# A convolution with spectral products and a recurrent layer: the start's loads and stores on two queues, and other buffers for the next image's statistics

## The chip, the cores and the metric

The kernel runs on one core of a Trainium2 chip. The metric is device time in microseconds (us) of one execution; lower is better. The engines are TensorE (PE in the profile, its weight loads PEld), VectorE (DVE), ScalarE (ACT), GpSimd (POOL) and SyncE (SP). SP, ACT and POOL issue DMAs; each has a queue of its own.

## The reference, cut to what matters

x is 4 images x 64 channels x 256 x 256, float32. Two layers with residuals follow one another, each after a group norm `_gn` over pairs of channels of one image:

```python
x = x + _L0_conv_ref(_gn(x), w1, w_dw, w_out, ln_w, ln_b)
x = x + _L1_conv_ref(_gn(x), w_ih, w_hh, b_ih, b_hh)
```

The first layer is a 1x1 convolution to 384 channels, a depthwise 3x3 convolution, a split into q, k and v of 128 channels, the circular convolution of q and k in patches of 8 x 8 (by FFTs), a layer norm over the channels, a product with v, and a 1x1 convolution back to 64 channels. The second is a GRU that runs along the image's columns.

What matters here is that `_gn` needs mean and variance of a whole image before its first value can be normalized.

## The kernel before, in words

**The program's order.** Every instruction is kept in program order on its engine (`InOrder`; all of them therefore carry line L157 in the profile, and rows are told apart by their tiles). Semaphores and the places of tiles come from the tile framework. A pool with `bufs=n` lends n buffers for a tag; a new tile waits until a buffer is free. A pool that is closed gives its memory to what is allocated later, which then waits for the last readers of the old tiles.

**The start (lines 214 to 257).** `bt` holds the taps as matrices, `wd` the depthwise weights; PE makes of them the matrices `ts` (100 partitions x 384 x 64), ACT copies them out of PSUM, and three DMAs on POOL's queue store them to `t_all` in HBM (3200 KB each). Meanwhile SP loads image 0 in eight pieces `xc` of 128 partitions x 4096 (three buffers), two DMAs a piece: `piece` yields partitions 0 to 63 (channels of the image's upper half), then 64 to 127. VectorE takes BATCH_NORM_STATS2 of each piece's eight stretches into `bn0` and aggregates into `st0`. `norm_of_pieces` makes scale and shift `sc0` of it. Then ACT issues the GRU's weight loads (`wi`, `wh`, `bias_sb`).

**The blocks (lines 273 to 693).** 32 blocks (n) of 32 columns, eight an image. Each holds its input in four tiles `xq` (loaded on POOL's queue, normalized by ACT or VectorE). In the loop over n:
- `pointwise(n, 0, unit)`, 16 units: matmuls into the ring of PSUM banks `psring`, copied to `h` by ACT or VectorE.
- `finish(n - 1)`: the block before is completed in four steps u: `residual` loads x into a work tile `xr` (SP), `gate` transposes and multiplies (work tiles `y`), `project` multiplies by w_out, adds to `xr`, takes its statistics and stores it to x1 (`store`, SP). The last project waits in `pending`, its store in `later`.
- `circular(n, 0, beside)`: four steps sp. Each transforms q and k (`transform`, with matrices `t` that SP streams back from `t_all`, four buffers), copies q to a work tile on ACT and forms two work tiles `pr` of products on VectorE; then it calls `beside(sp)`. `flush()` runs what is pending: after step 0 the last project of block n - 1, after step 2 the `inverse` of the first two steps (matmuls of `pr` by `g_sb`, copied to `z`).
- `pointwise(n, 1, unit)`, `circular(n, 1, beside)` with the first statistics of `layer_norm(n)`, `pointwise(n, 2, unit)` with the loads of the next `xq`, and `values` with the rest of the layer norm and the next `normalize`.

**Work tiles.** `work` lends from one pool of seven buffers (tag `wk`, 128 x 1024 float32). `q`, `k`, `pr`, `xr`, `y`, `lnm` and the next image's `seen` all come from it. The layer norm's own statistics `lnst` (128 x 768) are in the pool `big`, one buffer.

**The next image's statistics.** In the 24 blocks n < 24, `look(n, k, t)` loads a quarter (four columns of each half) of the matching piece of the next image on POOL's queue, in two DMAs, and `count(n, k, t)` takes two BATCH_NORM_STATS2 of it. `seen0` is looked at before `circular(n, 0)` and counted in its step 1; `seen1` is looked at before `pointwise(n, 1)`, counted and looked at anew at units 8 and 14, and counted for the last time in `circular(n, 1)`.

**The second layer (from line 700)** follows with pools of its own.

Of the kernel before, what the change touches and what calls it, by code (L numbers as in the profile page):

```python
# [19 lines left out]
P = 128  # L20
# [63 lines left out]
def norm_of_pieces(nc, st, t, psum, eps, sc):  # L84

    m_all, d, total, mean = t[:, 128:136], t[:, 136:144], t[:, 144:145], t[:, 145:146]
    nc.vector.tensor_copy(m_all, st[:, :, 0])
    nc.vector.tensor_reduce(total, m_all, mybir.AxisListType.X, ALU.add)  # L90
    yield
    pm = psum()
    nc.tensor.matmul(pm, lhsT=t[:, 0:P], rhs=total, start=True, stop=True)
    nc.vector.tensor_copy(mean, pm)
    nc.vector.tensor_tensor(d, m_all, mean.to_broadcast([P, 8]), ALU.subtract)
    nc.vector.tensor_tensor(d, d, d, ALU.mult)
    nc.vector.tensor_tensor(d, d, st[:, :, 1], ALU.add)
    nc.vector.tensor_reduce(total, d, mybir.AxisListType.X, ALU.add)
    yield
    pv = psum()  # L100
    nc.tensor.matmul(pv, lhsT=t[:, 0:P], rhs=total, start=True, stop=True)
    nc.scalar.activation(sc[:, 1:2], pv, AF.Sqrt, bias=eps, scale=1.0)
    nc.vector.reciprocal(sc[:, 1:2], sc[:, 1:2])
    nc.vector.scalar_tensor_tensor(sc[:, 0:1], mean, -1.0, sc[:, 1:2], ALU.mult, ALU.mult)
    yield
# [57 lines left out]
def tile_conv_then_gru(  # L163
# [42 lines left out]
    def piece(of, b, i, w, n):  # L206

        for half in range(2):
            w0 = half * (W // 2) + i * (W // 16) + w
            yield slice(half * C, (half + 1) * C), of[b, :, w0 : w0 + n, :].rearrange("c w h -> c (w h)")  # L210
# [6 lines left out]
    with tc.tile_pool(name="xa", bufs=3) as xa, tc.tile_pool(name="sta", bufs=1) as sta, tc.tile_pool(  # L217
        name="bps", bufs=1, space=PSUM
    ) as bps:
        bt = sta.tile([P, 32, HALO], F32, tag="bt", name="bt")  # L220
        wd = sta.tile([P, HID], F32, tag="wd", name="wd")
        for i in range(4):
            nc.scalar.dma_start(bt[32 * i : 32 * i + 9], taps[i])
            nc.sync.dma_start(wd[32 * i : 32 * i + 9], w_dw)
        avg4 = sta.tile([P, 1024], F32, tag="avg4", name="avg4_0")
        nc.sync.dma_start(avg4[:, 0:P], avg2)
        ts = sta.tile([HALO, 3 * P, NS], F32, tag="ts", name="ts")
        banks = bps.tile([P, 8, 512], F32, tag="b", name="psb")
        for i in range(32):
            kind, s = i // 16, i % 16  # L230
            c0, num = 2 * P * kind, 2 * P - P * kind
            ps = banks[0:HALO, 4 * (i % 2) : 4 * (i % 2) + 4, 0:num]
            for k in range(4):
                at = slice(32 * k, 32 * k + 9)
                nc.tensor.matmul(
                    ps[:, k],
                    lhsT=bt[at, i, :],
                    rhs=wd[at, c0 : c0 + num],
                    start=True,
                    stop=True,  # L240
                    tile_position=(32 * k, 0),
                )
            nc.scalar.copy(ts[:, c0 : c0 + num, 4 * s : 4 * s + 4], ps.rearrange("p s c -> p c s"))
        for i in range(3):
            nc.gpsimd.dma_start(
                t_all[i].rearrange("n p k -> p n k"),
                ts[:, i * P : (i + 1) * P].rearrange("p (n c) k -> p n (c k)", n=8),
            )
        for i in range(8):
            xc = xa.tile([P, 4096], F32, tag="xc", name=f"xc_{i}")  # L250
            for at, of in piece(x, 0, i, 0, 16):
                nc.sync.dma_start(xc[at], of)
            for k in range(8):
                nc.vector.bn_stats(bn0[:, k, :], xc[:, 512 * k : 512 * k + 512])
            nc.vector.bn_aggr(st0[:, i, :], bn0)
        for _ in norm_of_pieces(nc, st0, avg4, lambda: banks[:, 0, 0:1], eps, sc0[:, 0]):
            pass
    wi = const.tile([P, 9, C], F32, tag="wi", name="wi")
# [14 lines left out]
    with ExitStack() as s:  # L273
# [14 lines left out]
        def work(name, shape=(P, 1024)):  # L288
            return wk.tile(list(shape), F32, tag="wk", name=name)

        h = big.tile([HALO, P, NP], F32, tag="h", name="h")
        z = big.tile([P, NP, NS], F32, tag="z", name="z")
        v = big.tile([P, NP, NS], F32, tag="v", name="v")
        xq = {}

        def load(n, jq):
# [159 lines left out]

        def layer_norm(n):

            st = big.tile([P, 2, NP // 2, 6], F32, tag="lnst", name=f"lnst_{n}")

            def statistics(a, p0, p1):

                for p in range(p0, p1):
                    nc.vector.bn_stats(
                        st[:, a, p, :],
                        z[:, 2 * p : 2 * p + 2, 32 * a : 32 * a + 32].rearrange("p n f -> p f n"),
                    )

            for i in range(4):
                statistics(0, 16 * i, 16 * i + 16)  # L470
                yield
            statistics(1, 0, 8)
            yield
            statistics(1, 8, 50)
            yield
            statistics(1, 50, NP // 2)
            m = work(f"lnm_{n}", (P, 8, NP))
            total, mean, d, var, rstd = m[:, 0], m[:, 1], m[:, 2:4], m[:, 4], m[:, 5]
            by = st.rearrange("p a i (e k) -> p a (i e) k", e=2)
            nc.vector.tensor_tensor(total, by[:, 0, :, 1], by[:, 1, :, 1], ALU.add)  # L480
            yield
            pm = psum()
            nc.tensor.matmul(pm[:, 0, 0:NP], lhsT=hh_sb, rhs=total, start=True, stop=True)
            nc.vector.tensor_copy(mean, pm[:, 0, 0:NP])
            nc.vector.tensor_tensor(
                d,
                by[:, :, :, 1],
                mean.rearrange("p (x n) -> p x n", x=1).to_broadcast([P, 2, NP]),
                ALU.subtract,
            )  # L490
            nc.vector.tensor_tensor(d, d, d, ALU.mult)
            nc.vector.scalar_tensor_tensor(d, by[:, :, :, 2], 1.0 / 32, d, ALU.mult, ALU.add)
            nc.vector.tensor_tensor(var, d[:, 0], d[:, 1], ALU.add)
            yield
            pv = psum()
            nc.tensor.matmul(pv[:, 0, 0:NP], lhsT=hh_sb, rhs=var, start=True, stop=True)
            nc.scalar.activation(rstd, pv[:, 0, 0:NP], AF.Sqrt, bias=eps, scale=1.0)
            nc.vector.reciprocal(rstd, rstd)
            yield
            for u in range(4):  # L500
                for g in range(2):
                    at = slice(g * NJ + 16 * u, g * NJ + 16 * u + 16)
                    for part, what in ((mean, ALU.subtract), (rstd, ALU.mult)):
                        nc.vector.tensor_tensor(
                            z[:, at, :],
                            z[:, at, :],
                            part[:, at].rearrange("p (n x) -> p n x", x=1).to_broadcast([P, 16, NS]),
                            what,
                        )
                    yield  # L510
# [82 lines left out]
                    xr[g * C : (g + 1) * C],  # L593
                )

        def look(n, k, t):

            for at, of in piece(x, n // 8 + 1, n % 8, 4 * k, 4):
                nc.gpsimd.dma_start(t[at], of)

        def count(n, k, t):
            for i in range(2):
                nc.vector.bn_stats(bn0[:, 2 * k + i, :], t[:, 512 * i : 512 * i + 512])
            if k == 3:
                nc.vector.bn_aggr(st0[:, n % 8, :], bn0)

        def finish(n):

# [14 lines left out]
        for n in range(NBLK + 1):  # L623
# [4 lines left out]
            if n == NBLK:  # L628
                for _ in norm:
                    pass  # L630
            if n:
                finish(n - 1)
            if n == NBLK:
                flush()
                later.pop()()
                break
            more = n // 8 + 1 < B
            if more:
                seen = work(f"seen0_{n}")
                look(n, 0, seen)  # L640
            circular(n, 0, lambda sp: count(n, 0, seen) if more and sp == 1 else None)
            if more:
                seen = work(f"seen1_{n}")
                look(n, 1, seen)
            for unit in range(16):
                pointwise(n, 1, unit, unit in (5, 8, 11, 14))
                if more and unit in (8, 14):
                    count(n, unit // 7, seen)
                    look(n, unit // 7 + 1, seen)
            flush()  # L650
            norm = layer_norm(n)

            def beside(sp):
                next(norm)
                if more and sp == 1:
                    count(n, 3, seen)

            circular(n, 1, beside)
            image = None
# [264 lines left out]
```

## Time and profile before

| what | value |
|---|---|
| runs of the kernel before | 5904.98, 5915.67, 5931.4 us |
| median | 5915.67 us |
| the profiled execution: own time | 5924.77 us |
| the profiled execution: span from first to last instruction | 5923.0 us |
| granted TensorE clock | 0.992 |
| data moved by DMA | 818.09 MB, mean 138 GB/s |
| DMA packets' time on SP's queue (q1), share of 16 engines | 39.9% |
| DMA packets' time on POOL's queue (q0), share of 16 engines | 9.5% |

The profiled execution took 1.8 us more than its span. In the order of time the start lasts to about 140 us, the blocks to about 4330 us, the second layer to the end. A row of the profile reads: start, duration, engine, line, operation, tile written <- tiles read, shape, count, and in brackets how long the engine had stood idle and what ended that. An engine's name with a q is its sequencer, which issues DMAs. A busy share is an average over stages with different limits.

### The profile page before, as it was taken

Reading aid. Unit: us, or ns where it says so; the run is one execution under the profiler, and the core shown is the slowest. Engines: PE = TensorE matmul, PEld = TensorE weight load, DVE = VectorE, ACT = ScalarE, POOL = GpSimd, SP = SyncE. Lnnn points to the kernel's source line nnn. Section 1 sums busy time; section 2 is a strip of 40 time slices with the busy share of each in tenths; the row PEclk is TensorE's granted clock in tenths of the full one; section 3 lists DMA queues with packets and bytes.
Section 4 is the critical chain, followed back from the end, with each engine's and each line's share of the span. In section 5 each row is a group of like instructions: output and inputs, shape, how many; then the busy total and the mean of one; then the engine's idle time right before and its main releaser. Section 6 shows DMA issues by size and latency. Waiting matters only on the chain. (4 is left out here: it accounts for less than half of the span.)

```text
span 5923.0 us, 279366 instructions
## 1 busy us (share of the span) xinstructions
PE 5513.2 (93%) x127196; PEld 4736.6 (80%) x127196; DVE 4090.4 (69%) x9592; ACT 3466.3 (59%) x4604; POOL 499.7 (8%) x797
## 2 busy tenths in 40 slices
PE   2999999999999999999999999999979999999998
PEld 1888887888887888778878887887868888888887
DVE  2676776777667777776767776666766666676666
ACT  2556565665655666556566665656645555555555
POOL 0000000000000000000000000000001211121211
PEclk9999999999999999999999999999989999999999
DMA  8455555555555555555555545444454444444442
GB/s 223 132 160 142 154 151 155 152 141 160 151 147 149 157 155 141 147 162 146 153 146 154 145 127 142 133 131 136 123 119 112 113 112 110 113 114 113 111 113 78
DMA packets 561921, 818.09 MB, mean 138 GB/s; under 512 B 41352, under 2 KB 435372, under 8 KB 559676
## 3 DMA queue, kind: packets, MB, share of 16 engines
q1 hardware_dynamic: 520152, 633.59, 39.9%
q0 software_dynamic: 37776, 165.24, 9.5%
q8 instruction: 996, 16.32, 1.2%
q10 hardware_dynamic: 2808, 1.38, 0.1%
q14 instruction: 189, 1.55, 0.1%
HBM read 622.46 MB, written 144.05 MB: 129 GB/s over the span
## 5 line engine op out<-in xcount | busy, mean ns | idle before, releaser
L157 PEld LDWEIGHTS psring<-h,t 100*32 100x32 f32 x40960 | 1334.8, 115 | 300.4 <-issue 176.2
L157 PE MATMUL psring<-h,t 100*32 100x128 f32 x40960 | 1445.7, 274 | 113.0 <-issue 39.4
L157 PE MATMUL psring<-w_sb,xq 64*100 64x128 f32 x24576 | 1396.9, 271 | 58.1 <-POOL xq L157 44.1
L157 PEld LDWEIGHTS psring<-w_sb,xq 64*100 64x100 f32 x24576 | 1352.7, 163 | 117.9 <-issue 48.1
L157 ACT COPY h<-psring 100x1024 f32<-100x1024 f32 x1274 | 1204.0, 1026 | 156.8 <-PE psring L157 150.4
L157 DVE TENSOR_TENSOR pr<-psring,q 128x512 f32<-128x512 f32 (+1 forms) x576 | 463.0, 856 | 299.1 <-PE psring L157 230.8
L157 DVE BATCH_NORM_STATS2 lnst<-z 128x6 f32<-128x64 f32 x4096 | 544.8, 212 | 117.6 <-ACT z L157 117.6
L157 DVE TENSOR_TENSOR z<-z,lnm 128x1024 f32<-128x1024 f32 x512 | 612.6, 1217 | 8.7
L157 ACT COPY q<-psring 128x1024 f32<-128x1024 f32 x256 | 259.2, 1013 | 586.5 <-PE psring L157 351.2
L157 ACT ACTIVATE n<-n,bias_sb 128x288 f32<-128x288 f32 (+7 forms) x510 | 259.8, 509 | 572.7 <-DVE n L157 572.7
L157 ACT COPY z<-psring 128x2048 f32<-128x2048 f32 x128 | 238.9, 1866 | 463.3 <-PE psring L157 458.3
L157 PE MATMUL psring<-pr,g_sb 32*64 32x512 f32 x8192 | 497.5, 602 | 5.9 <-issue 5.7
L157 ACT ACTIVATE y<-psring,ln_sb 128x512 f32<-128x512 f32 x512 | 371.9, 780 | 199.7 <-PE psring L157 196.0
L157 DVE COPY h<-psring 100x1024 f32<-100x1024 f32 x262 | 320.3, 1223 | 193.5 <-PE psring L157 189.4
L157 PE MATMUL psni<-st,wi 64*64 64x144 f32 (+7 forms) x12240 | 440.9, 270 | 7.4 <-issue 6.7
L157 PE MATMUL pshr<-st,wi 64*64 64x144 f32 (+7 forms) x12240 | 434.0, 270 | 13.4 <-DVE st L157 12.9
L157 PE MATMUL pshz<-st,wi 64*64 64x144 f32 (+7 forms) x12240 | 439.4, 270 | 3.9 <-issue 3.5
L157 DVE TENSOR_TENSOR g<-xn,n 128x288 f32<-128x288 f32 (+7 forms) x510 | 217.4, 426 | 325.5 <-ACT n L157 325.5
L157 POOL TENSOR_TENSOR raw<-raw,st 128x512 f32<-128x512 f32 x256 | 303.4, 1185 | 1212.0 <-DVE st L157 522.0
L157 DVE TENSOR_TENSOR y<-psring,y 128x1024 f32<-128x1024 f32 x256 | 312.2, 1220 | 122.1 <-ACT y L157 118.8
L157 PEld LDWEIGHTS pshr<-st,wi 64*64 64x64 f32 x12240 | 362.1, 133 | 16.5 <-issue 16.0
L157 PEld LDWEIGHTS psni<-st,wi 64*64 64x64 f32 x12240 | 363.1, 133 | 14.3 <-issue 11.4
(97 smaller groups left out, 6984.0 us busy)
## 6 DMA issues: line engine op xcount, KB each, us to landing
t<-t_all SPq DMA_DIRECT2D x768, 400.0 KB
xq<-in_xh POOLq DMA_DIRECT2D x128, 800.0 KB, 4.6
xr<-in_x SPq DMA_DIRECT2D x256, 256.0 KB
x<-xr SPq DMA_DIRECT2D x256, 256.0 KB
seen<-in_x POOLq DMA_DIRECT2D x192, 256.0 KB, 4.1
raw<-x SPq DMA_DIRECT2D x128, 256.0 KB
raw<-x SPq DMA_DIRECT2D x256, 128.0 KB
xt<-xn SPq DMA_DIRECT2D x256, 128.0 KB
```

Source lines behind the costliest of these rows:

```text
L157: return self.tc.keep_in_program_order(got(*args, **kwargs))
```

## The change

Three parts. First, `bt` is loaded on SP's queue, behind `wd`, where it was on ACT's. Second, the two halves of each `xc` piece go out on SP's and POOL's queue, and the stores of `ts` come after them in the program, each cut into two halves of four matrices, one for each queue. Third, the next image's statistics: `lnst` is one tile for all blocks, and its first 512 values a partition serve as `seen`, two columns at a time, for the first half of a piece; the second half goes through one work tile `four`, four columns at a time. There are six looks a block (12 DMAs) instead of four (8 DMAs), and still eight BATCH_NORM_STATS2. The first look stands before `finish(n - 1)`; counts are at steps 0 and 3 of `circular(n, 0)`, at unit 8 and after unit 15 of `pointwise(n, 1)`, and in step 1 of `circular(n, 1)`.

```diff
         for i in range(4):
-            nc.scalar.dma_start(bt[32 * i : 32 * i + 9], taps[i])
             nc.sync.dma_start(wd[32 * i : 32 * i + 9], w_dw)
+            nc.sync.dma_start(bt[32 * i : 32 * i + 9], taps[i])
...
-        for i in range(3):
-            nc.gpsimd.dma_start(
-                t_all[i].rearrange("n p k -> p n k"),
-                ts[:, i * P : (i + 1) * P].rearrange("p (n c) k -> p n (c k)", n=8),
-            )
         for i in range(8):
             xc = xa.tile([P, 4096], F32, tag="xc", name=f"xc_{i}")
-            for at, of in piece(x, 0, i, 0, 16):
-                nc.sync.dma_start(xc[at], of)
+            for queue, (at, of) in zip((nc.sync, nc.gpsimd), piece(x, 0, i, 0, 16)):
+                queue.dma_start(xc[at], of)
...
+        for i in range(3):
+            for k, queue in enumerate((nc.sync, nc.gpsimd)):
+                queue.dma_start(
+                    t_all[i, 4 * k : 4 * k + 4].rearrange("n p k -> p n k"),
+                    ts[:, i * P + 64 * k : i * P + 64 * k + 64].rearrange("p (n c) k -> p n (c k)", n=4),
+                )
...
+        lnst = big.tile([P, 2, NP // 2, 6], F32, tag="lnst", name="lnst")
...
-            st = big.tile([P, 2, NP // 2, 6], F32, tag="lnst", name=f"lnst_{n}")
+            st = lnst
...
-        def look(n, k, t):
-
-            for at, of in piece(x, n // 8 + 1, n % 8, 4 * k, 4):
+        seen = lnst.rearrange("p a i k -> p (a i k)")[:, 0:512]
+
+        def look(n, w, t):
+
+            for at, of in piece(x, n // 8 + 1, n % 8, w, t.shape[1] // H):
                 nc.gpsimd.dma_start(t[at], of)
-        def count(n, k, t):
-            for i in range(2):
-                nc.vector.bn_stats(bn0[:, 2 * k + i, :], t[:, 512 * i : 512 * i + 512])
-            if k == 3:
-                nc.vector.bn_aggr(st0[:, n % 8, :], bn0)
+        def count(n, w, t):
+            for i in range(t.shape[1] // 512):
+                nc.vector.bn_stats(bn0[:, w // 2 + i, :], t[:, 512 * i : 512 * i + 512])
...
+            if n < NBLK and n // 8 + 1 < B:
+                look(n, 0, seen)
             if n:
                 finish(n - 1)
...
+            def beside_first(sp):
+                if more and sp in (0, 3):
+                    count(n, 2 * (sp // 3), seen)
+                    look(n, 2 * (sp // 3) + 2, seen)
+
+            circular(n, 0, beside_first)
             if more:
-                seen = work(f"seen0_{n}")
-                look(n, 0, seen)
-            circular(n, 0, lambda sp: count(n, 0, seen) if more and sp == 1 else None)
-            if more:
-                seen = work(f"seen1_{n}")
-                look(n, 1, seen)
+                four = work(f"seen_{n}")
+                look(n, 8, four)
             for unit in range(16):
                 pointwise(n, 1, unit, unit in (5, 8, 11, 14))
-                if more and unit in (8, 14):
-                    count(n, unit // 7, seen)
-                    look(n, unit // 7 + 1, seen)
+                if more and unit == 8:
+                    count(n, 4, seen)
+                    look(n, 6, seen)
+                    count(n, 8, four)
+                    look(n, 12, four)
+            if more:
+                count(n, 6, seen)
...
                 if more and sp == 1:
-                    count(n, 3, seen)
+                    count(n, 12, four)
+                    nc.vector.bn_aggr(st0[:, n % 8, :], bn0)
```

## The prediction

> **What bounds the kernel now.** I read the profile from the whole to the part: busy shares first, then the start in stretches and in order of time, then the 32 blocks, then one block with the next image's statistics beside one without.
>
> The page's first line gives the engines' busy time and share of the span.
>
> ```profile
> PE 5513.2 (93%) x127196; PEld 4736.6 (80%) x127196; DVE 4090.4 (69%) x9592; ACT 3466.3 (59%) x4604; POOL 499.7 (8%) x797
> ```
>
> TensorE (PE) is the bound almost everywhere. A change that leaves PE's work alone gains only where PE stands still: before its first block, and in gaps inside the blocks. Next, the start in stretches (columns: length; busy time of PE, PEld, DVE, ACT and POOL with instruction counts; clock, DMA share, GB/s):
>
> ```profile
> 25.00:45.00 20.00, 17.91 (x148) 7.61 (x146) 11.18 (x20) 16.84 (x19) 1.77 (x2) 1.00 1.03 216
> 55.00:80.00 25.00, 0.00 (x0) 0.00 (x0) 12.55 (x22) 0.00 (x0) 0.94 (x1) 1.00 1.01 250
> 90.00:97.00 7.00, 0.00 (x0) 0.00 (x0) 4.40 (x8) 0.00 (x0) 0.00 (x0) 1.00 1.00 330
> 136.00:142.00 6.00, 1.63 (x16) 1.63 (x18) 0.00 (x0) 1.72 (x1) 0.34 (x2) 1.00 1.03 326
> ```
>
> The DMA engines are full in all four, yet move different amounts. The x loads alone (SP, half the partitions at a time) get 216 GB/s; with the matrices' stores beside them on POOL's queue, 250; the stores nearly alone, 330; the xq loads (128 partitions, POOL) beside t loads (SP), 326. What follows the loads, in order of time:
>
> ```profile
> 92.60 4.84 DVE L157 BATCH_NORM_STATS2 bn<-xc 128x6 f32<-128x512 f32 x8 [4.40 <-DMA xc<-in_x]
> ...
> 128.52 7.54 SPq L157 DMA_DIRECT2D t<-t_all  x4
> 129.31 2.16 POOL L157 DMA_DIRECT2D xq<-in_xh  x4 [73.37 <-DMA wi<-in_w_ih]
> 138.14 1.72 ACT L157 ACTIVATE xq<-xq,sc 128x1600 f32<-128x1600 f32 x1 [35.95 <-DMA wi<-in_w_ih]
> 140.37 0.96 PE L157 MATMUL psring<-w_sb,xq 64*100 64x128 f32 x6 [39.83 <-POOL xq L157]
> ```
>
> The last x piece lands at 92.60. The last store is issued at 54.94 and takes 73.5 us, so it lands at 128.4; only then do SP and POOL go on, because the tiles that they load lie where ts lay. (The wi load that is named ends in the same stretch; SP's t load does not need it.) PE's first block follows 12 us after the last store. So the start is set by two bodies of DMA: 16.8 MB of x, then the rest of 9.8 MB of stores.
>
> Now the blocks: blocks 8 to 22 (with the next image's statistics) and 24 to 30 (without), each counted from its first copy out of psring into h.
>
> ```profile
> 1174.40:3136.80 1962.40, 1898.63 (x37506) 1600.00 (x37504) 1409.30 (x3280) 1186.70 (x1188) 102.64 (x247) 0.99 0.55 151
> 3269.70:4173.00 903.30, 876.73 (x17502) 739.35 (x17500) 620.71 (x1464) 553.65 (x555) 18.51 (x58) 1.00 0.49 137
> ```
>
> That is 1962.40 / 15 = 130.83 us a block against 903.30 / 7 = 129.04. DVE has 5.3 us more work a block with the statistics (93.95 against 88.67) but idles over 36 us in either; 1.79 us reach the end. Where, VectorE shows in order of time in circular(n, 0) of block 16 and of block 29:
>
> ```profile
> 2255.89 1.23 DVE L157 TENSOR_TENSOR pr<-psring,q 128x1024 f32<-128x1024 f32 x1 [1.12 <-PE psring L157]
> 2260.45 1.29 DVE L157 TENSOR_TENSOR pr<-psring,q 128x512 f32<-128x512 f32 x2 [3.33 <-DMA x<-xr]
> 2261.65 1.28 DVE L157 TENSOR_TENSOR xr<-psring,xr 128x512 f32<-128x512 f32 x2
> ...
> 2268.31 2.42 DVE L157 TENSOR_TENSOR pr<-psring,q 128x1024 f32<-128x1024 f32 x3 [0.19 <-issue]
> ```
>
> ```profile
> 3951.97 2.42 DVE L157 TENSOR_TENSOR pr<-psring,q 128x1024 f32<-128x1024 f32 x3 [1.12 <-PE psring L157]
> ...
> 3957.46 2.42 DVE L157 TENSOR_TENSOR pr<-psring,q 128x1024 f32<-128x1024 f32 x3 [0.15 <-PE psring L157]
> 3961.10 2.42 DVE L157 TENSOR_TENSOR pr<-psring,q 128x1024 f32<-128x1024 f32 x3 [1.22 <-PE psring L157]
> ```
>
> In block 16 the second product of step sp = 0 waits 3.33 us until the store of an earlier xr lands: seen0 has shifted the seven work buffers by one, so that product gets xr's buffer. From first to third group it takes 12.42 us against 9.13. Block 16 lasts 128.5 us, block 29 126.7.
>
> **The start, step by step.** *x loads.* Each piece's halves go out on SP and POOL together. SP begins x behind the wd, bt and avg loads, at about 6 us (bt's four are 0.46 MB); POOL at 1.5, with 1.0 MB by then at 216. Left: 16.8 + 0.5 - 1.0 = 16.2 MB. The rate of two queues of loads that fill 128 partitions lies between 250 (the second queue a side stream) and 326 (xq beside t); I take 310, nearer to the row of loads. 16.2 / 0.310 = 52 us: x ends at 58, not 92.6. VectorE keeps up: 8 x (4.84 + 0.37) = 42 us.
>
> The trace thus says that a second queue adds to 216 GB/s. The Trainium skill says otherwise ("DMA: Bandwidth & Descriptors", Rules for kernel authors): it advises against splitting a transfer into two for disjoint partition halves, since both run on the same 16 engines. By that rule x would still end at 92.6 and the start would be slower by 13. The same skill ("SBUF — State Buffer", the DMA port swizzle) lets 64 partitions reach half of the ports, 8 x 27.2 = 218 GB/s, which 216 agrees with; it adds that two transfers can't be fused, which 250 and 326 speak against.
>
> *Stores.* They are now queued behind x on both queues, in halves of 1200 packets of 4 KB. SP's t loads, of the same shape, run ten packets at a time in the trace (from 129.5 to 133.5 us), POOL's stores some 15. So the busiest DMA engines get 1200 / 10 + 7 x 12 = 204 packets, where all on POOL gave 7 x 24 = 168: the split balances worse. A packet took 0.193 us (88 to 95 us) to 0.253 (120 to 129); at 0.225 that is 46 us, and the last store lands at 58 + 46 = 104 instead of 128.4: **-24 us**. Ends: 326 and 0.193 give 55 + 39 = 94 (-34); 250 and 0.253 give 71 + 52 = 123 (-5).
>
> Behind them all stays as it is: xq, normalize, PE 12 us later. ACT's 13 weight loads, issued from 100.69 to 130.65 now, come before the first normalize on ACT's queue; they start near 70, and since SP and ACT take completion semaphores in turn (the x load of 13.18 us waited for that of a bt load), some must wait for SP's stores. I cost them nothing, since xq needs 9 us after the stores; without that cover each late us counts in full. The ts copies end at 54.65 even if bt is no earlier, before x does.
>
> **The blocks, step by step.** No seen0: the work buffers of circular(n, 0) come in the order of block 29. I take the whole difference, 23 blocks (1 to 23) x 1.79 = **-41 us**; ends: 0, and -45, if blocks 1 to 23 (first copies at 256.8 and 3269.7, so 131.00 each) all came down to 129.04. The statistics stay, so what they add in their new places:
> - count(n, 0) at sp = 0, one BATCH_NORM_STATS2 of 0.68, stands before the last project of the block before. In block 29 the second group of products would end at 3960.5; PE's inverse starts at 3960.9, so it is hidden by 0.4. If not: up to 0.68 x 23 = 16 us.
> - Three at unit 8 (2.03 us; two now). VectorE idles 1.40 before each h copy there, so unit 11's copy is 0.65 late; its psring slot is wanted at unit 15. Nothing.
> - count(n, 6) after unit 15: its look leaves about 4.5 us earlier, and landing took 3.4 to 5.1 in block 16. At most 0.6 us, before an idle of 4.9. Nothing.
> - POOL issues 12 DMAs a block for 8, 0.515 us each. Each look after the first waits on VectorE, and behind it on POOL stand only looks, until xq in chunk 2. look(n, 0) waits for the last read of lnst in layer_norm(n - 1), long done.
> - The q of sp = 1 now gets the buffer of xr 2, whose store must land within about 5 us; the blocks from 24 on show no such wait of ACT worth over 3.2 us in total.
>
> Sum: 5924.8 (this execution's own time, 1.8 over its span of 5923.0) - 24 - 41 = 5860. It lies 9.1 above the median of the runs, so on that scale: **5851 us**.
>
> **Rivals.**
> 1. *Two queues move x no faster.* For it: DMA share 1.03 with one queue. Against: 250 in the second row. Then 95 (SP starts x 3 us later) + 46 = 141: +13 - 41, that is 5888.
> 2. *The blocks' wait moves instead of going*: q of sp = 1, or the third group, waits for an xr store beside the new looks. For it: 5 to 6 us from issue to landing. Against: blocks 24 to 30. Then -24 alone: 5892.
> 3. *Slower: PE's instructions come late.* They arrive by DMA too (queue q8, 16.32 MB), and PE stands still inside a run of matmuls without any wait (1.45 us in block 28's inverse; 54 such gaps, longest 3.0). More and smaller looks now fall into circular(n, 0), among t loads and xr stores. Two more such gaps a block at up to 3.0 cost 23 x 6.0 = 138: 5989. It decides from 65 / 23 = 2.8 us a block. Against: counted in the trace, such gaps take 1.5 us a block with looks and 1.2 without.
>
> **How the numbers follow.** As forecast 0.62 (its own range 5837 to 5886); rival 1, 0.14; rival 2, 0.14; rival 3, 0.10. Its ends are -34 - 45 and -5 - 25 (41 less the count's 16). The range reaches 7 us further down, for PE's gaps (up to 3.0 us each) that will fall differently, and up over rivals 1 and 2: 5830 to 5900. A difference of 0.5% (30 us) is about what a measurement of this kernel can tell from no change. Faster by more (under 5886): nearly all of the forecast's case and half of what rivals 1 and 2 spread over, 0.72; within, 0.19; slower, 0.09.
>
> **What would show it.** Last bn<-xc near 58 (else rival 1); PE's first matmul on xq near 116; DVE's waits for DMA x<-xr gone (rival 2: on ACT q instead); blocks 8 to 22 near 129.0 us; PE gaps without a wait no more than now (rival 3). Wrong if x runs at 216, if SP's ten-engine half of the stores lands after 123, or if a block stays at 130.8.

## The result and the profile after

The changed kernel takes 5917.59 us (median of 12 runs, 5908.87 to 5927.15); the kernel before took 5915.55 beside it (12 runs, 5904.98 to 5939.05). The ratio of the runs is 0.9999 (1.0003 by the two medians), 95% interval 0.9986 to 1.0012: no difference that can be measured, where 5851 (5830 to 5900) was forecast. The profiled execution of after took 5909.25 us (span 5907.5), 8 below its median, while that of before lay 9 above its own: of the 15.5 us between the two profiles nothing may be given to the change as such.

TensorE's work is what it was:

```profile
PE 5498.9 (93%) x127196; PEld 4727.6 (80%) x127196; DVE 4089.6 (69%) x9592; ACT 3469.9 (59%) x4604; POOL 556.3 (9%) x901
```

The start, in the same stretches as before:

```profile
25.00:45.00 20.00, 16.10 (x122) 6.93 (x122) 9.18 (x16) 13.72 (x15) 0.52 (x1) 1.00 0.84 174
55.00:80.00 25.00, 2.47 (x32) 1.31 (x28) 13.85 (x24) 2.77 (x5) 3.58 (x5) 1.00 1.02 233
90.00:97.00 7.00, 0.00 (x0) 0.00 (x0) 6.07 (x12) 0.00 (x0) 0.00 (x0) 1.00 1.01 387
136.00:142.00 6.00, 0.00 (x0) 0.00 (x0) 0.00 (x0) 0.00 (x0) 0.00 (x0) 1.00 0.17 45
```

The first two stretches move 174 and 233 GB/s, not 310, but neither is x on two queues alone: SP sends no x before 27.84, and stores run beside x from 73 on. Between the two, x is alone on both queues:

```profile
45.00:58.00 13.00, 11.34 (x136) 6.74 (x128) 6.76 (x13) 10.38 (x18) 1.03 (x2) 1.00 0.99 222
```

With full DMA engines two queues of halves move 222 GB/s, hardly more than the 216 of one queue. The fourth row above is the worst: the DMA engines stand nearly idle (share 0.17) while all the other engines wait. In order of time, some of the rows of SP, POOL, VectorE and PE:

```profile
1.48 1.71 POOL L157 DMA_DIRECT2D xc<-in_x  x3
27.43 0.36 SPq L157 DMA_DIRECT2D avg<-in_avg  x1
27.84 45.09 SPq L157 DMA_DIRECT2D xc<-in_x  x8
72.97 44.46 SPq L157 DMA_DIRECT2D t_all<-ts  x3
73.30 2.55 POOL L157 DMA_DIRECT2D t_all<-ts  x3
92.08 4.84 DVE L157 BATCH_NORM_STATS2 bn<-xc 128x6 f32<-128x512 f32 x8 [0.86 <-DMA xc<-in_x]
...
142.73 2.17 POOL L157 DMA_DIRECT2D xq<-in_xh  x4 [66.88 <-DMA t<-t_all]
156.23 4.16 PE L157 MATMUL psring<-w_sb,xq 64*100 64x128 f32 x36 [56.22 <-POOL xq L157]
```

SP issues its first x load at 27.84, not at 6; the last piece lands at 92.08, as it did before (92.60). The stores, which began at 43 before, are issued from 73 on, and SP needs 44 us to issue its three. PE's first xq matmul comes 15.9 us later than before (156.23 against 140.37). These are single profiles: in the five kernels here that load x in halves on SP alone (before, stats_only, stats_late, x_near_halves and stores_after, below) it comes at 138.40 to 145.25. What held SP, from its waits in the first 160 us (us in total, times, longest):

```profile
SPq L157 <- DMA wi<-in_w_ih: 43.1, 1, 43.1
...
SPq L157 <- DMA wo_sb<-in_w_out: 11.7, 1, 11.7
SPq L157 <- DMA g_sb<-in_g: 9.4, 1, 9.4
```

None of these three tiles is SP's: they are ACT's small loads. SP waits for a completion semaphore that ACT's load holds: the trace has SP's fourth bt load wait for the semaphore that was given to `g_sb`, and its avg load for that of `wo_sb`. With the four bt loads on its queue SP stands behind these two until 27.43, and its third store, issued at 117.2, behind the first `wi` load. That store still landed no later than POOL's last one (141.7 and 141.9).

The blocks 8 to 22 and 24 to 30:

```profile
1181.95:3126.53 1944.58, 1884.86 (x37507) 1589.64 (x37504) 1407.47 (x3280) 1188.25 (x1188) 135.24 (x307) 1.00 0.55 152
3260.60:4161.17 900.57, 878.30 (x17503) 740.71 (x17500) 621.04 (x1464) 554.01 (x555) 18.61 (x58) 1.00 0.49 137
```

That is 129.64 a block with the next image's statistics (130.83 before) and still 128.65 without (129.04). The wait that was to go is gone. VectorE's waits for the store of xr in blocks 8 to 22, before:

```profile
DVE pr L157 <- DMA x<-xr: 42.8, 15, 3.8
```

and after:

```profile
DVE pr L157 <- DMA x<-xr: 6.9, 11, 1.1
```

circular(n, 0) of block 16 in VectorE's order of time after:

```profile
2259.40 2.42 DVE L157 TENSOR_TENSOR pr<-psring,q 128x1024 f32<-128x1024 f32 x3 [1.12 <-PE psring L157]
2261.73 0.69 DVE L157 BATCH_NORM_STATS2 bn<-lnst 128x6 f32<-128x512 f32 x1
2262.33 1.27 DVE L157 TENSOR_TENSOR xr<-psring,xr 128x512 f32<-128x512 f32 x2
...
2265.25 2.35 DVE L157 TENSOR_TENSOR pr<-psring,q 128x1024 f32<-128x1024 f32 x3
2269.10 1.23 DVE L157 TENSOR_TENSOR pr<-psring,q 128x1024 f32<-128x1024 f32 x1 [1.49 <-PE psring L157]
```

The first to the third group now takes 9.70 us (12.42 before, 9.13 in the old block 29). But the second group starts at once behind the project and its statistics, with no idle time before it: the count at step 0 has pushed it.

So in the profiles the start lost 12.9 us (block 0 begins at 161.57, not 148.72), and the 31 blocks up to block 31 took 24.6 less; but 2.7 of these lie in blocks 24 to 30, which the change hardly touches, and 2.2 in block 0. By the runs' medians loss and gain are equal.

### The profile page after: what moved, and what is told of

Same layout as the page of the kernel before. It is cut to its first block, busy times and chain, and to the rows that moved or that the text cites. A ratio compares the mean times of both kernels' runs of the same rounds, so it can differ in the third digit from the quotient of the medians.

```text
span 5907.5 us, 279517 instructions
## 1 busy us (share of the span) xinstructions
PE 5498.9 (93%) x127196; PEld 4727.6 (80%) x127196; DVE 4089.6 (69%) x9592; ACT 3469.9 (59%) x4604; POOL 556.3 (9%) x901
## 5 line engine op out<-in xcount | busy, mean ns | idle before, releaser
L157 PE MATMUL psring<-pr,g_sb 32*64 32x512 f32 x8192 | 485.2, 601 | 7.7 <-issue 7.7
```

Source lines behind the costliest of these rows:

```text
L157: return self.tc.keep_in_program_order(got(*args, **kwargs))
```

## The experiments

For the start three theories stood against each other: two queues of halves are no faster, since what limits x is how many partitions one DMA spans; or two queues would be fast, but for SP's wait for ACT's small loads; or x matters little, and the stores' split or place costs. For the blocks: the removed wait was worth what I took, or much less. "1 run" means one time, without an interval. Before took 5915.58 beside the first four kernels (29 runs, 5900.47 to 5931.51) and 5910.58 beside the next four (1 run).

**stats_only**: before's start with the change's third part. The edit is the third part of the diff alone.

> Before's start with the change's third part alone (lnst as seen, one work tile four). Theory A (the third part gains in the blocks what the profile after shows, 131.00 to 130.13 us over blocks 1 to 23, and the start loses it): PE's first matmul on xq at 140.4 as before, blocks 1 to 23 near 130.1 each, total 20 us under before (10 to 30). Rival B (the lower block times of the one profile after are chance; blocks spread by 126 to 135 us anyway): total within 6 us of before.

Measured: 5914.02, ratio 0.9997 (0.9984 to 1.0009). The third part beside the old start gains nothing that can be measured: 2 us less, between 9 less and 5 more. Theory A's 20 us were a miss. So was its first xq matmul at 140.4: it came at 145.25, with the start unchanged.

**start_only**: before's blocks with the change's first and second part.

> Before's blocks with the change's first two parts alone (bt on SP, x halves on SP and POOL, stores behind them in halves). Theory A: SP's first x load at about 27 us again, last bn<-xc near 92, last store near 142, PE's first matmul on xq near 153, total 13 us over before (8 to 20). Rival B (start costs nothing, a later first block is made up later): total within 5 us of before.

Measured: 5933.85, ratio 1.0035 (1.0023 to 1.0047): the new start costs 21 us (14 to 28; 8 to 20 were expected). Its profile has SP's first x load at 27.38, last bn<-xc at 92.38, the third SP store at 117.0 and the first xq matmul at 153.18, as in after.

**bt_on_act**: after with the taps back on ACT's queue.

```diff
+            nc.scalar.dma_start(bt[32 * i : 32 * i + 9], taps[i])
             nc.sync.dma_start(wd[32 * i : 32 * i + 9], w_dw)
-            nc.sync.dma_start(bt[32 * i : 32 * i + 9], taps[i])
```

> After with bt back on ACT's queue, all else as changed. Theory A (SP's x was held back because SP's queue stands in order behind DMAs whose completion semaphores come late, as small packets take turns with POOL's 16 KB ones): SP's first x load at 3 to 6 us, both halves together from then. If two queues then move x at 310 GB/s as I forecast, last bn<-xc near 60 and PE's first xq matmul near 118. Rival C (x is bound by something that a second queue and the other partitions don't lift; 233 GB/s in the stretch from 55 to 80 us of after): 16.8 MB / 0.233 = 72 us, last bn<-xc near 77 to 80, last store near 128, PE near 140.

Measured (1 run): 5904.44. SP now starts x at 2.87 and POOL at 1.47, both queues run from the first us on, and yet the windows and the last piece read:

```profile
25.00:45.00 20.00, 3.42 (x6) 1.21 (x6) 13.43 (x24) 1.28 (x1) 1.03 (x2) 1.00 1.05 183
55.00:80.00 25.00, 21.22 (x210) 10.97 (x208) 13.83 (x25) 19.80 (x28) 3.02 (x5) 1.00 1.02 227
```

```profile
89.68 4.84 DVE L157 BATCH_NORM_STATS2 bn<-xc 128x6 f32<-128x512 f32 x8 [1.54 <-DMA xc<-in_x]
```

SP's stall is not the whole story: without it two queues still need until 89.68 for x, later than either theory had it. The first xq matmul comes at 145.55: of the 15.9 us that it was late in after, 10.7 go with the taps' queue; the 5.2 that stay are within the spread of the old start (138.40 to 145.25). The stores come late for another reason than in after: they wait for the matrices themselves, not only for x loads in front of them. POOL's last store shows it:

```profile
79.74 0.83 POOL L157 DMA_DIRECT2D t_all<-ts  x1 [9.77 <-ACT ts L157]
```

Beside two queues of x the taps on ACT's queue land at 33 to 48 us (13 to 24 in before). The copies into ts that the first stores need end at 67.7, the last copy at 79.45 (54.65 in before). So the stores start late in either place of the taps: at 73 in after, behind x loads, and at 68 and 79 here, behind late taps.

**stats_late**: stats_only with the first count of circular(n, 0) in step 1.

```diff
-                if more and sp in (0, 3):
+                if more and sp in (1, 3):
```

> As stats_only, but the first count stands in step 1 of circular(n, 0) instead of step 0, behind the last project of block n - 1. Theory A' (the count in step 0 delays project's adds, and with them a PSUM slot that PE waits for, 0.3 to 0.7 us in most blocks): PE gaps that VectorE's pr or bn end go from about 0.4 us a block to under 0.1, total another 5 to 10 us under stats_only. Rival B' (that wait only takes the place of another): the same as stats_only within 4 us.

Measured: 5909.56, ratio 0.9983 (0.9973 to 0.9993), 10 us less than before. The interval overlaps with that of stats_only; the same edit comes again below.

**x_rows128**: before with each x piece loaded by one DMA over 128 partitions on SP. Image rows go to partition 2 x channel + half; the averaging matrix is left in the old order, so image 0 gets scales of other channels.

```diff
-            for at, of in piece(x, 0, i, 0, 16):
-                nc.sync.dma_start(xc[at], of)
+            nc.sync.dma_start(xc, x[0].rearrange("c (a w) h -> (c a) (w h)", a=2)[:, i * 4096 : (i + 1) * 4096])
```

> Before, but each piece of image 0 comes as one DMA of 128 partitions on SP (row 2c + half holds channel c's half, 16 KB a row, 128 KB apart in HBM), so the statistics of image 0 are averaged over other pairs of rows and its scale is that of other channels. Port theory (one DMA over 64 partitions is held at 216 GB/s because it reaches half of SBUF): 300 GB/s or more, 16 KB packets near 0.75 us, last bn<-xc by 60 to 66. Source theory (x's rows, a multiple of 128 KB apart in HBM, are read at 210 to 235 GB/s however they are issued): packets stay over 1.0 us, last bn<-xc at 80 or later. Packet theory (16 KB rows are slow as such): as the source theory here.

Measured (1 run): 5892.09.

```profile
25.00:45.00 20.00, 17.92 (x153) 7.96 (x152) 19.73 (x34) 16.59 (x20) 2.14 (x2) 1.00 0.98 369
55.00:80.00 25.00, 1.15 (x4) 1.00 (x4) 8.38 (x22) 1.54 (x2) 0.57 (x1) 1.00 0.96 258
```

```profile
58.00 4.85 DVE L157 BATCH_NORM_STATS2 bn<-xc 128x6 f32<-128x512 f32 x8 [1.27 <-DMA xc<-in_x]
```

One queue, the same bytes, the same three buffers: 369 GB/s where halves got 216, with the DMA share near 1 in both. x ends at 58.00, the very time that I had forecast for two queues. The first xq matmul comes at 119.77.

**x_near_halves**: as x_rows128 with the rows of a piece lying next to each other in HBM, but in two DMAs of 64 partitions on SP.

```diff
+            of = x[0, 8 * i : 8 * i + 8].rearrange("c (k w) h -> (c k) (w h)", k=16)
+            for half in range(2):
+                nc.sync.dma_start(xc[half * C : (half + 1) * C], of[half * C : (half + 1) * C])
```

> Before, but the pieces take rows that lie next to each other in HBM (8 channels of image 0, cut into 128 rows of 16 KB), in two halves of 64 partitions on SP as before; the statistics of image 0 are therefore those of other values. Source theory: 16 KB packets drop under 0.85 us, x moves at 280 GB/s or more, last bn<-xc by 70. Port theory and packet theory: packets 1.0 to 1.25 us, 216 GB/s, last bn<-xc at 88 to 92.

Measured (1 run): 5901.64, with x as slow as before (last bn<-xc at 91.37, first xq matmul at 140.84), so the 9 us to before are no effect of the start. They show no other effect either: these are single runs, and the 29 runs of before lie 31 us apart.

```profile
25.00:45.00 20.00, 17.92 (x150) 7.68 (x148) 10.21 (x19) 16.77 (x19) 1.85 (x2) 1.00 1.00 211
```

Rows that lie next to each other are as slow as rows far apart, and packets of 16 KB are no bar, since x_rows128 has them too. The 64 partitions of each DMA are what is left, or that there are two DMAs of 1 MB instead of one of 2 MB. No run here separates these two, but size alone is unlikely: xq's DMAs of 0.8 MB, over 128 partitions, were in the row of 326 GB/s.

**two_queues_act**: before with x on two queues, taps on ACT, and the three stores whole on POOL behind x.

> Before's blocks; bt on ACT, x halves on SP and POOL, the stores behind them whole on POOL (3 DMAs). Against bt_on_act this undoes the SP half of the stores alone. Engine theory (a DMA over 100 partitions runs on ten DMA engines, SP's always on the same ten, POOL's on ten that move on from DMA to DMA, so the busiest engine has 200 packets of 4 KB with halves on SP and 160 with all on POOL): stores end 36 us after x (x ends near 90), last store near 126, PE's first xq matmul near 138. Rival (two queues store faster, the loss is only that they start after x): last store at 133 or later, PE at 145 or later.

Measured (1 run): 5913.3. x ends at 84.98, the stores are issued at 67 to 79, and the first xq matmul comes at 152.76. If the split of the stores had been the cost, it would have come near 138, with the last store near 126. Without the split the last store lands even later, at 138.7 (bt_on_act: 133.3); that theory falls. As in bt_on_act the taps land late (37 to 47 us), and the stores at 67 and 79 wait for the copies into ts.

**stores_after**: before with the stores behind x in the program, on POOL.

> Before, but the three stores stand behind the x loads on POOL's queue. It prices the place of the stores alone. In before 1.4 MB of 9.8 went beside x at no cost to x. Expected: x as before (last bn<-xc 90 to 93), last store 3 to 6 us later than 128.4 (131 to 135), PE's first xq matmul at 143 to 147. Rival (engines are full anyway, what the stores took beside x they took from x): x ends 4 to 6 us earlier and PE starts at 140 as before.

Measured (1 run): 5914.78; first xq matmul at 140.21. This was a miss: with x on SP, POOL has nothing else to wait for and issues the stores at 43.0, 44.2 and 54.7 as before. In this kernel the place in the program costs nothing by itself; it can cost only where the queue holds x loads that wait for a buffer.

The last four were run together, 6 runs each, beside 5918.71 for before (11 runs). All load x as x_rows128 does, and a second averaging matrix in that row order gives every channel its own scale.

**rows_fair**: nothing else changed.

> The kernel before with each x piece of the first image loaded by one transfer over all 128 partitions on SP, and with an averaging matrix in that row order, so that every channel gets its own scale; nothing else changed. Ports theory (one transfer over 128 partitions is what lifts x, a second queue isn't): last bn<-xc near 58, last store near 105, first xq matmul near 121, 20 us less, ratio about 0.9965. Rival (the 20 us of the one run of x_rows128 were that run's own): first xq matmul near 120 again but a time within 5 us of before, since something behind it gives the gain back.

Measured: 5878.5, ratio 0.9939 (0.9919 to 0.9959): 36 us less (24 to 48). The first xq matmul comes at 112.61, 28 us earlier than in before. The rival falls; 20 us less were expected.

**rows_late**: with stats_late's blocks.

> rows_fair with the change's third part (one buffer for the statistics, one work tile) and its first count in step 1 of the circular convolution instead of step 0, as in stats_late. If start and blocks are independent: 20 and 10 us less, about 5885, ratio about 0.995. Rival (stats_late's 10 us came of how its start lay to its blocks, or of chance between builds): about 5895, no better than rows_fair.

Measured: 5868.83, ratio 0.9916 (0.9898 to 0.9934): 50 us less, the fastest kernel here. It beats rows_fair by about 10 us, as stats_late beat before; the two intervals overlap.

**rows_late_stores2**: with the stores in halves on ACT's and POOL's queue.

```diff
-            nc.gpsimd.dma_start(
...
+            for k, queue in enumerate((nc.scalar, nc.gpsimd)):
+                queue.dma_start(
```

> rows_late with each of the three stores of the matrices in two halves, on ACT's queue and POOL's, ahead of x as in before. If the stores are bound by their ten engines and by x's packets beside them, two queues change nothing: last store near 105, time within 5 us of rows_late. Rival (one queue's issue bounds them): last store near 85 to 95, 10 to 20 us less than rows_late.

Measured: 5884.04, ratio 0.9939 (0.9923 to 0.9955). SP's first t load comes at 101.10 (rows_late: 100.21): splitting the stores brings nothing at the start, and the whole is 15 us slower by the medians, though the intervals overlap. In the profile block 0 takes 110.7 us (rows_late 106.9) and blocks 1 to 23 take 130.48 each (130.14). The granted clock accounts for the blocks: without the time lost to it they take 129.89 and 129.84. Block 0 was not followed further.

**rows_after**: the change with x in one DMA per piece on SP and the taps on ACT; stores in halves on SP and POOL behind x, and the blocks, as the change has them.

> The changed kernel, with x by one transfer per piece over 128 partitions on SP, the taps back on ACT, stores in halves on SP and POOL behind x, as the change has them, and its blocks (first count in step 0). If what the change lost at the start was only that POOL's queue held x ahead of the stores while x was no faster: SP's and POOL's halves are issued at 43 to 58, last store 100 to 110, first xq matmul 115 to 125, about 20 us less than before by the start and up to 8 by the blocks: 5888 to 5896. Rival (halves on two queues are slow by themselves): last store 117 or later, first xq matmul over 130, 10 us less or none.

Measured: 5877.94, ratio 0.9934 (0.9917 to 0.9952): 39 us less than before.

```profile
57.05 4.85 DVE L179 BATCH_NORM_STATS2 bn<-xc 128x6 f32<-128x512 f32 x8 [0.93 <-DMA xc<-in_x]
...
97.36 9.50 SPq L179 DMA_DIRECT2D t<-t_all  x4
98.10 2.15 POOL L179 DMA_DIRECT2D xq<-in_xh  x4 [43.26 <-DMA t<-t_all]
109.20 3.10 PE L179 MATMUL psring<-w_sb,xq 64*100 64x128 f32 x26 [44.20 <-POOL xq L179]
```

With x really at 57, the last stores land about 97 (forecast 104 from x at 58) and PE starts at 109 (forecast 116). The steps of the start that stood behind x's rate were right to 7 us, in part by luck: the stores were to follow x, and here they began at 42 to 54, beside it. Against rows_fair, which has before's blocks, it gains nothing that can be measured (0.9934 and 0.9939).

## Why the prediction was wrong

**x's rate: the first step that failed.** I took 310 GB/s for halves on two queues, from the rows of 250 and 326. Neither row held two halves: 250 was one half at a time beside stores that read SBUF, and 326 was xq, whole DMAs over 128 partitions, beside t loads. The runs gave 211 to 218 GB/s for halves on one queue (25 to 45 us), 218 to 237 for halves on two (45 to 58 us) and 369 to 397 for one DMA over 128 partitions on one queue (25 to 45 us). For the start rival 1 was the right one, and the row that spoke for it (DMA share 1.03 with one queue) was the row to believe: with the engines already full, a second queue added next to nothing. Rival 1's 13 us more, with the 9 us that the blocks gained (below) in place of 41, give 5920 on the forecast's scale; 5917.59 was measured. The Trainium skill's rule that I set aside ("DMA: Bandwidth & Descriptors", Rules for kernel authors) says to use one 128-partition transfer instead of two for disjoint halves, and "SBUF — State Buffer" (Can I just issue two DMAs to hit both halves?) that two transfers can't be fused. The rates above agree with both. Which of their reasons holds, shared engines or shared ports, no run here separates.

**SP's waits for ACT's loads: costed at nothing.** I had SP begin x at 6 us, and wrote of late weight loads only that ACT's might wait for SP. It went the other way: SP waited 21 us for two of ACT's small loads in front of x, and then for `wi` ahead of its third store. Putting the taps back took 10.7 us off the first xq matmul (1 run, where one start spreads over 7 us) and brought x's end forward by only 2.4.

**Stores.** With the x that there was, the forecast's own rival gave 141 for the last store, and so 153 for PE; after had 142 and 156. That part of the arithmetic held in sum, in part by luck. From the end of x to the last store it had 46 us; after took 50, bt_on_act 44, two_queues_act 54 with whole stores, and rows_after 40 with stores that had begun beside x.

**The blocks: the term of 41 us was mis-sized.** The mechanism was right (the waits for x<-xr fell from 42.8 to 6.9 us, and blocks 1 to 23 from 130.99 to 130.13), but the whole difference between blocks 8 to 22 and 24 to 30 was never due to it. Three things were in it.

First, the granted clock. It falls to 0.50 for 3.41 or 6.83 us at a time, and blocks 8 to 22 of before had five such stretches, 20.5 us in all, where 24 to 30 had none. Half of that is lost: 10.2 / 15 = 0.68 of the 1.79 us a block. The rows that I showed said it: the third figure from their end is the clock (0.99 and 1.00), and PE's busy time was 126.58 us a block against 125.25. Block 13 of before, with 6.83 us at half clock, beside block 14 with none:

```profile
1824.48:1958.69 134.21, 128.68 (x2503) 108.05 (x2500) 93.92 (x219) 79.07 (x81) 6.73 (x16) 0.97 0.53 147
1958.69:2087.00 128.31, 126.14 (x2503) 107.09 (x2500) 93.80 (x219) 79.09 (x80) 7.18 (x18) 1.00 0.56 154
```

And in rows_fair 10.2 us of it (5.1 of the 12 us of difference) fell on block 28, which has no statistics at all, beside block 29:

```profile
3757.21:3895.62 138.41, 130.38 (x2503) 108.91 (x2500) 88.72 (x210) 79.08 (x81) 2.58 (x8) 0.96 0.46 128
3895.62:4021.88 126.26, 124.43 (x2503) 105.43 (x2500) 88.72 (x210) 79.08 (x81) 2.58 (x8) 1.00 0.51 139
```

These stretches don't come at random. The clock's record moves in steps of 3.41 us. In blocks 1 to 30 of the 14 profiles all 97 falls come right after a step in which PE or PEld ran for 0.02 to 0.63 of the time (median 0.45); of the 15777 other steps at full clock 9 were under 0.5. The longest gap in that step was one without a named wait in 78 cases, the five of before's blocks 8 to 22 among them (1.5 to 3.0 us each), a wait for the next image's scale (VectorE's avg) in 15, and a wait for VectorE's xr or pr in 4. So a gap in PE is paid again in half clock behind it. The gaps without a named wait go with the instruction loads that rival 3 named: of the 320 over 0.9 us, 299 end 1.0 to 1.9 us after a packet of queue q8 has landed, where 13% of instants picked at random do. That late instructions cause them is likely, but no experiment here shows it.

Second, most of VectorE's wait never reached PE. Stretches in which neither PE nor PEld ran, ended by DVE's xr or pr, came to 0.57 us a block in before's blocks 1 to 23; those that DVE's pr or bn ended in after, to 0.40: 0.17 x 23 = 4 us. I read VectorE's rows and took the block's length for the price; the wait had to be followed to PE.

Third, the rest stays with the statistics: net of the clock, blocks 8 to 22 of after are still 1.14 us longer than its own 24 to 30 (before: 1.11). Of before's 1.11 us 0.46 are time in which neither PE nor PEld ran (4.20 against 3.74 us a block); the other 0.65 are longer running time. Net of the clock, blocks 1 to 23 last 130.19 us on average with before's blocks (seven kernels) and 129.81 with the change's (four; 129.94 in the three with the later count): 0.38 x 23 = 9 us instead of 41. The seven range over 0.6 us, so this is known to some 6 us.

**The count at step 0: not hidden, its price not shown.** I had 0.4 us of cover for 0.68. PEld's waits for VectorE in blocks 8 to 22 of after:

```profile
PEld psring L157 <- DVE pr L157: 5.9, 9, 1.1
...
PEld psring L157 <- DVE bn L157: 2.8, 3, 1.0
```

and of rows_late, with that count one step later:

```profile
PEld psring L179 <- DVE pr L179: 2.1, 7, 0.4
...
PEld psring L179 <- DVE bn L179: 0.7, 1, 0.7
```

Both pairs with the later count were faster, by 4 us (stats_late to stats_only) and 9 us (rows_late to rows_after, which differ in their stores too), neither alone outside its interval. The profiles don't show the gain in the blocks: net of the clock, blocks 1 to 23 go from 130.14 us to 130.08 in the first pair and from 129.67 to 129.84 in the second, since other gaps of PE grew by as much.

**Rivals 2 and 3** didn't decide it. ACT's q waits no longer for DVE's pr (153.4 us in blocks 8 to 22 before, 0.8 after). Instead the profile puts 38.6 us of its waits down to xr loads, 2.6 us a block where before had none. That is little more than the 2.3 in blocks 24 to 30 (16.1 us in seven), which have no looks, and no gap of PE there ended with ACT's q. PE's gaps without a named wait are 1.7 us a block in blocks 1 to 23 of both kernels.

**What stays open.** The parts don't add up exactly: the third part gains 2 us beside the old start (stats_only) and 21 beside the new one (start_only to after), each known to some 8 to 10 us. Much of the spread goes with the granted clock: the 29 runs of before average 5924.9 us at a clock of 0.991 (4 runs), 5917.0 at 0.992 (11), 5912.4 at 0.993 (9) and 5905.6 at 0.994 (3), where 0.001 of the clock is 5.9 us. As an estimate, with the time lost to the clock taken off each run, the third part gains 4 us beside the old start and 12 beside the new one, each to some 5, on both sides of the 9 from the profiles; the new start costs 16. Still open are the 0.65 us of longer running time, the cause of TensorE's gaps without a named wait, and whether ports or engines hold a DMA over 64 partitions.

## What to carry to other kernels

A row that shows full DMA engines at a low rate asks for another shape of the transfer, not for another queue: count the partitions that one DMA spans before splitting it. A wait on an engine that isn't the bound is worth only what of it ends idle time on the engine that is, so follow it there, and compare stages by busy time and granted clock before reading their difference as a wait. Where the clock falls, look at the engine's gaps just before it. A load moved to another queue brings that queue's order with it: what stood on it now waits for whatever the moved load waits for.

## What the runs showed of the hardware

- One DMA of 2 MB over 128 partitions ran at 369 to 397 GB/s (25 to 45 us, five profiles). DMAs of 1 MB over 64 partitions ran at 211 to 218 on one queue (25 to 45 us, five profiles) and at 218 to 237 on two (45 to 58 us, four profiles). From 25 to 45 us a packet of 16 KB took 0.61 us (median) in x_rows128 and 1.24 in x_near_halves.
- SP stood 43.1 us on a semaphore held by another queue's load that it did not use.
- Small loads beside x came late: the four tap loads of 0.1 MB landed at 33 to 48 us beside two queues of x (bt_on_act), at 13 to 24 beside one (before).
- The granted clock fell to half in 11 to 19 stretches in each of the 14 profiles, most of them of 3.41 us or a multiple, one of 30.7 to 34.1 us at the end of the blocks; 40 to 56 us of TensorE's time were lost in each. In the blocks a fall came after 3.41 us in which TensorE and its weight loads ran for 0.63 of the time or less.
- 299 of 320 gaps of TensorE over 0.9 us without a named wait, in blocks 1 to 30 of the 14 profiles, ended 1.0 to 1.9 us after a packet of the instruction queue had landed.
